# A fused attention and feed-forward layer on one core: the choice of path moved behind the fast path, and the first groups fed in another way

## The chip, the cores and the metric

The kernel runs on one core of a Trainium2 chip. A core has five engines that run side by side: TensorE (PE, matrix products), VectorE (DVE), ScalarE (ACT), GpSimd (POOL) and SyncE (SP, which only issues transfers here). The metric is the device time of one execution in microseconds. A group of transfers is issued from SP's queue or from ScalarE's queue, and an engine waits for another, or for a transfer, on a semaphore.

## The reference

The input x has shape (2, 256, 128, 128): batch, time, frequency, channels. Three residual steps follow each other, each behind a layer norm over the channels:

```
xt = _ln(x, ln_t_w, ln_t_b).transpose(0, 2, 1, 3)
x = x + _mha(xt, t_wi, t_bi, t_wo, t_bo, H_T, cm).transpose(0, 2, 1, 3)   # causal, over the 256 times
xf = _ln(x, ln_f_w, ln_f_b)
x = x + _mha(xf, f_wi, f_bi, f_wo, f_bo, H_F, bm)                         # band of 16, over the 128 frequencies
xn = _ln(x, ln_n_w, ln_n_b)
h = jax.nn.gelu(xn @ w1.T + b1, approximate=False)
x = x + (h @ w2.T + b2)
```

`_mha` is attention with four heads of 32 channels: queries, keys and values from one product with wi, scores divided by the root of 32, a mask, a softmax, the product with the values, and the product with wo. Everything is in float32. The inner width of the last step is 512.

## The kernel before

**Two paths.** A softmax is usually computed with the row's maximum subtracted. The kernel has a `shifted_path` that does so, and a `bounded_path` that leaves it out. The second is right where the weights bound the scores. The function `fold` folds the layer norm's weights into wi (`wf`), folds the biases (`bq`), and computes from these weights six sums (`tests`). They are compared with limits, and the outcome is one integer, `flag` (line 415 loads it into a register of every engine). A branch on it chooses the path (line 1263). In the runs shown the bounded path is taken.

**Groups.** The bounded path works on 128x512 tiles, called groups here: four rows of 128 tokens each. There are 128 groups of attention over time (class `OverTime`, called g0, g1 and so on below), then, in turns of eight, groups of attention over frequency (`OverBands`) and of the feed-forward step (`FeedForward`). A group goes through these methods:

- `load`: four transfers of 32 partitions each bring four groups' tokens at once (a quad).
- `statistics`: VectorE forms mean and variance (tiles `stats`, `mv`). `root_by_scalar`: ScalarE forms the inverse root as a logarithm and an exponential (`lnv`, `root`). `refine`: three small VectorE steps make it exact (`vy`, `rstd`).
- `normalize`: four VectorE instructions write the normalized tokens `xh`. `turn`: VectorE transposes blocks of 32x32 into `z`, and four transfers write z to DRAM (`turned`). `fetch`: one transfer reads it back with channels on the partitions (`xnT`). So a group is transposed by VectorE and two trips through DRAM.
- `queries_keys`, `take_query`, `take_key`: TensorE multiplies xnT with `wf`, ScalarE copies the results out as `qT` and `kT`. `values`, `take_values` give `v`.
- Scores, exponentials (`p`, by ScalarE), masks and sums (POOL), `weigh` (TensorE: sums of weights `rp` and outputs `op`), `invert`, `divide` (`oT`), `output` and `finish`.

**Order.** `run` (line 1109) writes the whole order out by hand. In one pass n of its loop it emits the steps of several groups: the scores of g(n), the queries of g(n+2), the fetch for g(n+3), the normalizing of g(n+4), the statistics of g(n+5), the roots of g(n+5). Passes below zero fill the pipeline. Instructions emitted through the wrapper `InOrder` keep this order on their engine, and an engine takes its list strictly from the front. TensorE's results go to eight banks of PSUM. The time groups use a fixed rotation of banks, the others take the next one in a ring (`turn_of_bank`).

**Start.** `load_constants` issues, on SP's queue, the small columns and rows and then the first quad (`x0`, four transfers of 256 KB), and on ScalarE's queue the weights. Then comes `fold`, then the branch. Inside the bounded path, in pass n = -4, `fold_rest` computes what is left of the folding (`wn`, `orow`, `b1`, `w1f`), and `warm` sends eight products of 128x384 that nobody reads through TensorE. All instructions that go through `InOrder` carry one line of the program in the profile (924 before), so groups of instructions are told apart by their tiles.

Of the kernel before, what the change touches and what calls it, by code (L numbers as in the profile page):

```python
# [28 lines left out]
RUN = 32  # L29
SAFE = 30.0  # L30
# [11 lines left out]
def load_constants(ctx, tc, x, t_wiT, t_woT, f_wiT, f_woT, w1T, w2T, cols, rows):  # L42
# [5 lines left out]
    k.const = const  # L48
    k.cols = const.tile([P, 16], F32, name="cols_sb")
    nc.sync.dma_start(k.cols, cols)  # L50
    k.rows = const.tile([P, 3, C], F32, name="rows_sb")
    for i in range(3):
        nc.sync.dma_start(k.rows[:, i, :], rows[i : i + 1, :].partition_broadcast(P).squeeze(1))


    k.x0 = const.tile([P, NT, NT, C], F32, name="x0")
    for i in range(NT):
        f = i // (T // P) * NT
        nc.sync.dma_start(k.x0[rows_of(i)], BoundedPath.of_times(x[0], i, slice(f, f + NT)))

    def weight(src, n, name):
        t = const.tile([P, n], F32, name=name)
        nc.scalar.dma_start(t, src)
        return t

    k.wiT = (weight(t_wiT, 3 * C, "t_wiT_sb"), weight(f_wiT, 3 * C, "f_wiT_sb"))
    k.woT = (weight(t_woT, C, "t_woT_sb"), weight(f_woT, C, "f_woT_sb"))
    k.w1T = weight(w1T, k.NI * P, "w1T_sb")
    k.w2T = const.tile([P, k.NI, C], F32, name="w2T_sb")
    nc.scalar.dma_start(k.w2T, w2T.rearrange("(j p) c -> p j c", p=P))  # L70
# [273 lines left out]
def fold(tc, k):  # L344

    nc = tc.nc
    const = k.const
    C = P  # L350
    scale = 1.0 / math.sqrt(D)
    tensor, vector, scalar = InOrder(tc, nc.tensor), InOrder(tc, nc.vector), InOrder(tc, nc.scalar)

    def col(i):
        return k.cols[:, i : i + 1]

    k.ones = const.tile([P, P], F32, name="ones")
    nc.vector.memset(k.ones, 1.0)
    k.wf, k.bq = [], []
    tests = const.tile([P, 6], F32, name="tests")  # L360
    with tc.tile_pool(name="foldp", bufs=2) as fp, tc.tile_pool(name="foldps", bufs=1, space=PSUM) as pp:
        scalar.preload_act_table_set(EXP_SET)

        bp = pp.tile([P, 2], F32, name="bp")
        for a in range(2):
            tensor.matmul(bp[:, a : a + 1], k.wiT[a][:, 0:C], col(5 * a + 1), start=True, stop=True)
        for a in range(2):
            c0 = 5 * a
            wf = const.tile([P, 3 * C], F32, name=f"wf{a}")
            vector.tensor_scalar(wf[:, 0:C], k.wiT[a][:, 0:C], col(c0), scale, ALU.mult, ALU.mult)  # L370
            vector.tensor_scalar(wf[:, C : 3 * C], k.wiT[a][:, C : 3 * C], col(c0), None, ALU.mult)
            bq = const.tile([P, 1], F32, name=f"bq{a}")
            vector.tensor_scalar(bq, bp[:, a : a + 1], col(c0 + 2), scale, ALU.add, ALU.mult)
            k.wf.append(wf)
            k.bq.append(bq)
        brs = []
        for a in range(2):
            brp = pp.tile([1, P], F32, name=f"brp{a}")
            tensor.matmul(brp, k.bq[a], k.ident, start=True, stop=True)
            br = fp.tile([1, P], F32, name="br")  # L380
            scalar.copy(br, brp)
            brs.append(br)

        for a in range(2):
            wf, wo = k.wf[a], k.woT[a]
            br = brs[a]
            gk = pp.tile([P, P], F32, name="gk", tag=f"gk{a}")
            tensor.matmul(gk, wf[:, C : 2 * C], wf[:, C : 2 * C], start=True, stop=True)
            gq = pp.tile([P, P], F32, name="gq", tag=f"gq{a}")
            tensor.matmul(gq, wf[:, 0:C], wf[:, 0:C], start=True, stop=False)  # L390
            tensor.matmul(gq, br, br, start=False, stop=True)
            gs = fp.tile([P, P], F32, name="gs")
            scalar.copy(gs, gk)
            vector.tensor_tensor(gs, gq, gs, ALU.mult)
            for h in range(H):
                r = rows_of(h)
                vector.tensor_reduce(tests[r, 3 * a : 3 * a + 1], gs[r, r], AX.X, ALU.add)
            for j, w in ((1, wf[:, 2 * C : 3 * C]), (2, wo)):
                sq = fp.tile([P, P], F32, name="sq")
                scalar.activation(sq, w, AF.Square, accum_out=tests[:, 3 * a + j : 3 * a + j + 1])  # L400
        tp = pp.tile([P, 6], F32, name="tp")
        tensor.matmul(tp, k.ones, tests, start=True, stop=True)
        ok = fp.tile([P, 6], F32, name="ok")
        for a in range(2):
            vector.tensor_scalar(
                ok[:, 3 * a : 3 * a + 1], tp[:, 3 * a : 3 * a + 1], SAFE * SAFE / (C * (C + 1)), None, ALU.is_le
            )
            vector.tensor_scalar(
                ok[:, 3 * a + 1 : 3 * a + 3], tp[:, 3 * a + 1 : 3 * a + 3], LARGE, None, ALU.is_le
            )  # L410
        allok = fp.tile([P, 1], F32, name="allok")
        vector.tensor_reduce(allok, ok, AX.X, ALU.min)
        flag = const.tile([P, 1], I32, name="flag")
        vector.tensor_copy(flag, allok)
    return nc.values_load(flag[0:1, 0:1], min_val=0, max_val=1)


# [10 lines left out]
class Group:  # L428
# [91 lines left out]
    def fetch(self):  # L520
        path = self.path
        self.xnT = path.work.tile([P, NT * P], F32, name="xnT")
        path.sync.dma_start(self.xnT, self.turned.rearrange("c a i x -> (c a) (i x)"))

# [404 lines left out]
class BoundedPath:  # L929
    def __init__(self, ctx, tc, k):  # L930
# [12 lines left out]
        self.sync = InOrder(tc, tc.nc.sync)  # L943
        self.dram = ctx.enter_context(tc.tile_pool(name="turns", bufs=3, space=DRAM))
        self.zero = 0.0
        self.once = once = ctx.enter_context(tc.tile_pool(name="once", bufs=1))
        self.eps = once.tile([P, 1], F32, name="eps")
# [121 lines left out]
    def fold_rest(self):  # L1069

        k, tensor, vector, scalar = self.k, self.tensor, self.vector, self.scalar
        C = P

        def col(i):
            return k.cols[:, i : i + 1]

        k.wn, k.orow = [], []
        for a in range(2):
            c0 = 5 * a

            bp = self.bank([P, 1], "bp")
            tensor.matmul(bp, k.wiT[a][:, 2 * C : 3 * C], col(c0 + 1), start=True, stop=True)
            bv = self.small.tile([P, 1], F32, name="bv")
            scalar.activation(bv, bp, AF.Identity, bias=col(c0 + 4))
            wn = self.once.tile([P, C], F32, name=f"wn{a}")
            scalar.mul(wn, k.woT[a], -1.0)
            k.wn.append(wn)
            orow = self.once.tile([P, C], F32, name=f"orow{a}")
            scalar.activation(orow, k.ones, AF.Copy, scale=bv)
            op = self.bank([P, C], "op")  # L1090
            tensor.matmul(op, orow, k.woT[a], start=True, stop=True)
            vector.tensor_tensor(orow, op, k.rows[:, a, :], ALU.add)
            k.orow.append(orow)
        b1p = self.bank([P, k.NI], "b1p")
        for j in range(k.NI):
            tensor.matmul(b1p[:, j : j + 1], k.w1T[:, j * P : (j + 1) * P], col(11), start=True, stop=True)
        k.b1 = self.once.tile([P, k.NI], F32, name="b1")
        vector.tensor_tensor(k.b1, b1p, k.cols[:, 12 : 12 + k.NI], ALU.add)
        k.w1f = self.once.tile([P, k.NI * P], F32, name="w1f")
        scalar.activation(k.w1f, k.w1T, AF.Copy, scale=col(10))  # L1100

    def warm(self):


        for _ in range(8):
            bank = self.bank([P, 3 * P], "warm")
            self.tensor.matmul(bank, self.k.ones, self.k.wf[0], start=True, stop=True)

    def run(self, x, out):
# [24 lines left out]
        self.scalar.preload_act_table_set(EXP_SET)  # L1134
        for n in range(-12, len(groups) + 2):
# [13 lines left out]
            if old is not None or new is not None:  # L1149
                time_scores(old, new)  # L1150
                b = self.banks
                Attention.place = dict(yp=b["b0"], rp=b["b3"], op=b["a1"], qp=b["a2"], kp=b["b1"], vp0=b["b0"], vp1=b["b2"])
            else:
                Attention.place = {}
# [19 lines left out]
            do_at(n + 3, OverTime, "fetch")  # L1174
# [8 lines left out]
            do_at(n + 4, OverTime, "normalize", "turn")  # L1183
# [11 lines left out]
            if n == -4:  # L1195
                self.fold_rest()
                self.warm()
# [4 lines left out]
            if bands[2] or turn:  # L1202
                do(n - 2, "output", "finish")
            do(n - 1, "divide")
# [15 lines left out]
            if n < 0:  # L1220
                do_at(n + 5, OverTime, "root_by_scalar", "refine")
            do_at(n, OverTime, "bias")
# [81 lines left out]
```

## Time and profile before

| what | us |
| --- | --- |
| median of three runs | 2664.97 |
| lowest and highest | 2662.14, 2665.03 |
| profiled execution: its own time | 2662.95 |
| its span | 2661.2 |
| TensorE busy in the span | 2630.1 (99%) |
| VectorE, ScalarE, POOL busy | 2140.1, 1841.8, 1947.3 |
| first queries of g0 begin | 28.27 |

The profile is one execution. Times count from the start of its span. A row of the timeline gives the start, the length, the engine, the line, the operation, the tile that it writes and those that it reads, shapes and count. Square brackets give the idle time of that engine before the row, and what ended it. PEld is the loading of weights into TensorE, which overlaps the products. Matmuls are pipelined and their ends are modelled, so starts are the safer numbers. A float32 product appears as two records.

### The profile page before, as it was taken

To read this page: it belongs to the slowest core of one execution; us is meant where nothing else is said; L and a number is where in the kernel's file an instruction comes from. 1 tells how busy PE (TensorE), PEld (TensorE's weight loads), DVE (VectorE), ACT (ScalarE), POOL (GpSimd) and SP (SyncE) were. 2 spreads that over 40 slices of the span, in tenths; PEclk is the share of its full clock that TensorE was granted. 3 is DMA by queue.
4 is the path that set the end of the run, shared out by engine and by line. 5 is a ranking of instruction groups with operands and counts; after the bars stand their busy time and mean duration, and the time that the engine had idled before them with its cause. 6 is when DMAs were issued, how large, how long until landed. Compare 5 with 4: busy or idle time off the path is not lost.

```text
span 2661.2 us, 156426 instructions
## 1 busy us (share of the span) xinstructions
PE 2630.1 (99%) x68662; PEld 1930.4 (73%) x68662; DVE 2140.1 (80%) x6429; ACT 1841.8 (69%) x3562; POOL 1947.3 (73%) x2297
## 2 busy tenths in 40 slices
PE   7999999999999999999999999999999999999998
PEld 5667667666676668778777687777777877777777
DVE  6988888888888897977868779678687796886874
ACT  6898999989989874664755746647557466475573
POOL 4999999999999986756667667666676676666762
PEclk9999999999999999999999999999999999999999
DMA  6655555555556454444444444444444454544533
GB/s 147 159 155 149 152 153 153 150 151 157 149 154 153 121 129 120 124 122 126 118 118 126 122 118 126 120 125 118 123 125 119 117 129 113 133 118 121 127 95 82
DMA packets 471510, 347.08 MB, mean 130 GB/s; under 512 B 43296, under 2 KB 405152, under 8 KB 470816
## 3 DMA queue, kind: packets, MB, share of 16 engines
q1 hardware_dynamic: 469568, 335.92, 49.0%
q8 instruction: 540, 8.85, 1.5%
q10 hardware_dynamic: 1248, 1.05, 0.2%
q14 instruction: 154, 1.26, 0.2%
HBM read 169.03 MB, written 167.77 MB: 127 GB/s over the span
## 4 chain that ended last, share of the span: by engine, by line
PE 86%; DVE 10%; DMA 2%; SPq 0%; issue 0%; ACT 0%; DVEq 0%; ACTq 0%
PE bank L924 86%; DVE xh L924 2%; DVE bank L924 2%; DVE z L924 1%; DVE u L924 1%; DVE oT L924 1%; DVE stats L924 1%; DVE x L924 1%; DMA xnT<-turned 1%; DMA turned<-z 1%; SPq L924 0%; DVE mv L924 0%; DMA x<-in_x 0%; DMA rows_sb<-in_rows 0%; ACT p L924 0%
## 5 line engine op out<-in xcount | busy, mean ns | idle before, releaser
L924 ACT ACTIVATE hT<-bank,b 128x512 f32<-128x512 f32 x512 | 346.9, 688 | 527.0 <-PE bank L924 496.3
L924 POOL TENSOR_SCALAR_AFFINE_SELECT pf<-pf 128x512 f32<-128x512 f32 x768 | 476.8, 635 | 178.5 <-ACT pf L924 152.2
L924 PEld LDWEIGHTS bank<-w2T_sb,hT 128*32 128x32 f32 x16384 | 498.2, 110 | 22.9 <-issue 16.7
L924 PE MATMUL bank<-xnT,w1f 128*32 128x512 f32 x4096 | 510.0, 592 | 0.0
L924 PE MATMUL bank<-w2T_sb,hT 128*32 128x128 f32 x16384 | 504.0, 273 | 0.2 <-ACT hT L924 0.2
L924 PE MATMUL bank<-xnT,wf 128*32 128x512 f32 x4096 | 492.5, 592 | 3.5 <-ACT p L924 3.0
L924 ACT ACTIVATE p<-bank 128x512 f32<-128x512 f32 (+1 forms) x1024 | 430.4, 495 | 65.0 <-PE bank L924 64.6
L924 POOL TENSOR_SCALAR_AFFINE_SELECT p<-p 128x1024 f32<-128x1024 f32 (+2 forms) x384 | 363.6, 947 | 81.2 <-ACT p L924 72.9
L924 DVE TENSOR_SCALAR xh<-x,mv,rstd 128x160 f32<-128x160 f32 x1040 | 404.4, 431 | 9.7
L924 PEld LDWEIGHTS bank<-wf,xnT 128*32 128x32 f32 x8192 | 243.6, 110 | 144.0 <-issue 103.2
L924 DVE TENSOR_TENSOR res<-bank,res 128x512 f32<-128x512 f32 x256 | 170.5, 666 | 218.8 <-PE bank L924 192.0
L924 PEld LDWEIGHTS bank<-xnT,w1f 128*32 128x32 f32 x4096 | 247.2, 110 | 128.2 <-issue 114.9
L924 POOL TENSOR_TENSOR p<-p,p 128x512 f32<-128x512 f32 x256 | 323.9, 1287 | 10.7
L924 DVE BATCH_NORM_STATS2 stats<-x 128x6 f32<-128x128 f32 x1536 | 329.5, 277 | 0.2 <-DMA x<-in_x 0.2
L924 POOL TENSOR_SCALAR rstd<-mv 128x4 f32<-128x4 f32 x248 | 56.3, 227 | 369.1 <-DVE mv L924 368.3
L924 PE MATMUL bank<-qT,kT 32*64 32x80 f32 (+4 forms) x16384 | 314.3, 273 | 2.4 <-ACT p L924 1.0
L924 PEld LDWEIGHTS bank<-qT,kT 32*64 32x64 f32 x16384 | 271.3, 131 | 54.5 <-ACT kT L924 50.3
L924 ACT ACTIVATE pf<-bank 128x512 f32<-128x512 f32 x512 | 266.7, 602 | 46.7 <-PE bank L924 44.1
L924 PE MATMUL bank<-wn,oT 128*32 128x128 f32 x8192 | 283.4, 274 | 0.7 <-DVE oT L924 0.7
L924 DVE STREAM_TRANSPOSE z<-xh 128x512 f32<-128x512 f32 x384 | 273.3, 712 | 13.2
L924 PE MATMUL bank<-wf,xnT 128*32 128x128 f32 x8192 | 276.7, 273 | 0.0
L924 POOL TENSOR_TENSOR rstd<-rstd,mhalf 128x4 f32<-128x4 f32 x248 | 256.6, 1035 | 20.7
(102 smaller groups left out, 3806.0 us busy)
## 6 DMA issues: line engine op xcount, KB each, us to landing
turned<-z SPq DMA_DIRECT2D x1536, 64.0 KB, 2.7
xnT<-turned SPq DMA_DIRECT2D x384, 256.0 KB, 3.1
x<-in_x SPq DMA_DIRECT2D x128, 256.0 KB, 4.4
x<-res SPq DMA_DIRECT2D x256, 128.0 KB, 2.6
x<-x SPq DMA_DIRECT2D x128, 256.0 KB, 4.2
out<-res SPq DMA_DIRECT2D x256, 128.0 KB, 2.5
w1T_sb<-in_w1T ACTq DMA_DIRECT2D x1, 256.0 KB, 5.7
w2T_sb<-in_w2T ACTq DMA_DIRECT2D x1, 256.0 KB, 7.0
```

The costliest lines, as they stand in the source:

```text
L924: return self.tc.keep_in_program_order(emit(*args, **kwargs))
```

## The change

The branch is moved to the end. The bounded path always runs. The shifted path follows only where the flag is zero, and writes the output again. The six sums and the flag are computed during the feed-forward stage.

Four other things change with it:

- The first quad is loaded group by group: g0's tokens first, then g1's, then g2's and g3's together. `cols` moves to ScalarE's queue, where the load of the activation tables stands behind the first weight.
- The first four groups (`TURNED`) are not transposed through DRAM. `normalize_flat` writes xh densely, `turn_by_tensor` multiplies it with the identity on TensorE, and ScalarE copies the result from PSUM into `xnT`.
- The folding is spread over VectorE, POOL and ScalarE and over several passes of the loop (`fold`, `fold_products`, `fold_biases`, `squares`, `fold_outputs`, `fold_rows`, `fold_hidden`). The second `wf`, `wn` and `w1f` are now made by POOL.
- The eight warm products use the identity and ones instead of a folded weight, and run at the very start: three, then the two small products of `fold_products`, then five.

```diff
+TURNED = 4
 def load_constants(...):
-    nc.sync.dma_start(k.cols, cols)
+    scalar.dma_start(k.cols, cols)
+    k.x0 = const.tile([P, NT, NT, C], F32, name="x0")
+    def tokens(g, n):
+        for i in range(NT):
+            f = i // (T // P) * NT + g
+            sync.dma_start(k.x0[rows_of(i), :, g : g + n], BoundedPath.of_times(x[0], i, slice(f, f + n)))
...
+    tokens(0, 1)
+    t_wi = weight(t_wiT, 3 * C, "t_wiT_sb")
+    scalar.preload_act_table_set(EXP_SET)
+    tokens(1, 1)
+    k.wiT = (t_wi, weight(f_wiT, 3 * C, "f_wiT_sb"))
+    k.woT = (weight(t_woT, C, "t_woT_sb"), weight(f_woT, C, "f_woT_sb"))
     k.rows = const.tile([P, 3, C], F32, name="rows_sb")
...
+    tokens(2, 2)
     k.w1T = weight(w1T, k.NI * P, "w1T_sb")
...
+    def normalize_flat(self):
+        path = self.path
+        self.xh = path.work.tile([P, NT, P], F32, name="xh", bufs=2)
+        for i in range(NT):
+            path.vector.tensor_scalar(
+                self.xh[:, i], self.src()[:, i], self.mv[:, i, 0:1], self.rstd[:, i : i + 1], ALU.subtract, ALU.mult
+            )
+
+    def turn_by_tensor(self, bank):
+        path = self.path
+        self.turned = path.bank([P, NT, NT, D], "turn", bank)
+        for i in range(NT):
+            path.tensor.matmul(
+                self.turned[:, i].rearrange("p i q -> p (i q)"), self.xh[:, i], path.k.ident, start=True, stop=True
+            )
+        self.xnT = path.work.tile([P, NT * P], F32, name="xnT")
+        path.scalar.copy(self.xnT.rearrange("p (i t q) -> p t i q", i=NT, q=D), self.turned)
...
+    def fold(self, a, engine):
+        engine.tensor_scalar(wf[:, 0:C], k.wiT[a][:, 0:C], col, 1.0 / math.sqrt(D), ALU.mult, ALU.mult)
+        engine.tensor_scalar(wf[:, C : 3 * C], k.wiT[a][:, C : 3 * C], col, None, ALU.mult)
...
+    def squares(self):
+        for a in range(2):
+            tensor.matmul(brp[0:1, a], k.bq[a], k.ident, start=True, stop=True)
+        scalar.copy(br, brp[0:1])
+        for a in range(2):
+            tensor.matmul(gk[:, a], wf[:, C : 2 * C], wf[:, C : 2 * C], start=True, stop=True)
+        scalar.copy(self.gs[:, 0], gk)
+        for a in range(2):
+            tensor.matmul(gq[a], wf[:, 0:C], wf[:, 0:C], start=True, stop=False)
+            tensor.matmul(gq[a], br[:, a], br[:, a], start=False, stop=True)
+            scalar.copy(self.gs[:, 1, a], gq[a])
...
+    def fold_outputs(self):
+        for a in range(2):
+            tensor.matmul(bp[:, a : a + 1], k.wiT[a][:, 2 * C :], k.cols[:, c0 + 1 : c0 + 2], start=True, stop=True)
+        for a in range(2):
+            scalar.activation(bv[:, a : a + 1], bp[:, a : a + 1], AF.Identity, bias=k.cols[:, c0 + 4 : c0 + 5])
+            scalar.activation(k.orow[a], k.ones, AF.Copy, scale=bv[:, a : a + 1])
+            tensor.matmul(self.orowp[:, a], k.orow[a], k.woT[a], start=True, stop=True)
+            self.gpsimd.tensor_scalar(k.wn[a], k.woT[a], -1.0, None, ALU.mult)
...
     def run(self, x, out):
+        self.warm(range(3))
+        self.fold(0, self.vector)
+        self.fold(1, self.gpsimd)
+        self.fold_products()
+        self.warm(range(3, 8))
         for n in range(-12, len(groups) + 2):
...
-            do_at(n + 3, OverTime, "fetch")
+            if n + 3 >= TURNED:
+                do_at(n + 3, OverTime, "fetch")
...
-            do_at(n + 4, OverTime, "normalize", "turn")
+            if n + 4 < TURNED:
+                do(n + 4, "normalize_flat")
+            else:
+                do_at(n + 4, OverTime, "normalize", "turn")
+            if n == -4:
+                groups[0].turn_by_tensor(4)
...
-            if n == -4:
-                self.fold_rest()
-                self.warm()
+            if n == -5:
+                self.fold_biases()
...
+            if n == len(groups):
+                self.bounded = self.nc.values_load(self.flag[0:1, 0:1], min_val=0, max_val=1)
             do(n - 1, "divide")
...
+            if n == -5:
+                self.squares()
+                self.fold_outputs()
+            if n == -4:
+                self.fold_rows()
+            for i in range(2):
+                if n == ff[i]:
+                    self.test(i)
+            if n == ff[2]:
+                self.verdict()
...
             do_at(n + 2, OverTime, "values", "take_values")
+            if 0 < n + 3 < TURNED:
+                groups[n + 3].turn_by_tensor(2 if n == -2 else self.banks["a1"])
+            if n == -2:
+                self.fold_hidden()
...
-    bounded = fold(tc, k)
-    with tc.If(bounded > 0) as cmp:
-        bounded_path(tc, k, x, out)
-    with cmp.Else():
+    bounded = bounded_path(tc, k, x, out)
+    with tc.If(bounded < 1):
         shifted_path(tc, k, x, out)
```

`test` and `verdict` hold the sums and comparisons that stood in `fold`. The third and fourth feed-forward groups run `test` (one product, four sums and two squares each), and the fifth runs `verdict`, whose one matmul is called `tp`.

## The prediction

> **What bounds the kernel now.** The page comes first: the busy line, then the chain that ended last.
>
> ```profile
> PE 2630.1 (99%) x68662; PEld 1930.4 (73%) x68662; DVE 2140.1 (80%) x6429; ACT 1841.8 (69%) x3562; POOL 1947.3 (73%) x2297
> ...
> PE 86%; DVE 10%; DMA 2%; SPq 0%; issue 0%; ACT 0%; DVEq 0%; ACTq 0%
> ```
>
> TensorE is the bound nearly everywhere, and the change leaves the order of its work untouched after the fourth group (the two kernels' lists of TensorE instructions agree there but for one matmul). So only the start can move. The timeline of the start, by engine (start, length, engine, instruction, wait before it):
>
> ```profile
> 13.09 0.15 DVE L924 CAST flag<-allok 128x1 int32<-128x1 f32 x1
> ...
> 14.33 0.87 DVE L924 BATCH_NORM_STATS2 stats<-x 128x6 f32<-128x128 f32 x4 [0.25 <-DMA x<-in_x]
> ...
> 23.51 0.34 PEld L924 LDWEIGHTS bank<-wf,ones 128*128 128x128 f32 x1 [0.30 <-issue]
> ...
> 24.15 0.34 PEld L924 LDWEIGHTS bank<-wf,ones 128*128 128x128 f32 x1 [0.30 <-issue]
> ...
> 24.79 2.94 PEld L924 LDWEIGHTS bank<-wf,ones 128*128 128x128 f32 x9 [0.30 <-issue]
> ```
>
> Nothing of the tokens is touched before the flag of 13.09 is read. The eight warm matmuls from 20.80 run 0.64 us per half (23.51 to 24.15), then 0.33 (2.94 over 9): the clock doubles near 25, 4.3 us after they began, although the clock shown by stretches is 1.00. Then TensorE alone:
>
> ```profile
> 20.80 7.53 PE L924 MATMUL bank<-wf,ones 128*128 128x384 f32 x16
> 28.27 1.93 PE L924 MATMUL bank<-xnT,wf 128*32 128x512 f32 x16
> ...
> 34.14 1.92 PE L924 MATMUL bank<-xnT,wf 128*32 128x512 f32 x16 [1.15 <-ACT p L924]
> ...
> 40.22 1.92 PE L924 MATMUL bank<-xnT,wf 128*32 128x512 f32 x16 [1.83 <-ACT p L924]
> ...
> 47.01 1.93 PE L924 MATMUL bank<-xnT,wf 128*32 128x512 f32 x16
> ...
> 54.95 2.23 PE L924 MATMUL bank<-xnT,wf 128*32 128x512 f32 x16 [0.56 <-DMA xnT<-turned]
> ```
>
> Each xnT,wf row opens a group's queries and keys: g0 at 28.27, then 5.87, 6.08, 6.79, 7.94 later. From g4 on nothing differs between the builds, so the question is when g4 starts, now 54.95. Finally ScalarE's rows of the first groups:
>
> ```profile
> 25.51 0.30 ACT L924 ACTIVATE lnv<-mv,eps 128x4 f32<-128x4 f32 x1 [4.82 <-DVE mv L924]
> 25.84 0.20 ACT L924 ACTIVATE root<-lnv 128x4 f32<-128x4 f32 x1
> 29.40 0.69 ACT L924 ACTIVATE qT<-bank,bq 128x512 f32<-128x512 f32 x1 [3.36 <-PE bank L924]
> ```
>
> The roots of g1 and g2 were done before g0's queries existed: the turn through DRAM left VectorE free to run ahead. That is what the change disturbs.
>
> **What the Trainium skill says.** "TensorE: Matmul & The Clock Gate", What's actually happening: the clock runs at half until a busy window of 3413 ns has passed, windows being free-running; the 4.3 us above agree. Same page, Architectural detail: ScalarE and VectorE are strict FIFO. The trace agrees: qT above stands behind both roots. "ScalarE: Activation LUTs", What ACT_TABLE_LOAD costs: an ACTIVATE without pointer operand takes 186 ns + 0.833 N, 0.61 for N = 512; kT's copy took 0.58.
>
> **The change, step by step** (times from the span's start; X is the moment g0's xnT is ready).
>
> *To the end of the warm matmuls.* Gone from the front: the squares' tests, the flag, the branch (13.09 to 13.9). Tokens of g0 come first; four 64 KB issues of 0.44 (turned<-z, 1.77 for 4) and 2.7 to land give about 5. TensorE needs only ident: 1.6. Three warm matmuls at 1.28 end at 5.5; bp needs f_wi, which landed 3.5 after its issue; it is now behind t_wi and a table load of 1.28, so issued 1.7 to 3.0, landing 5.2 to 6.5. Five more warm matmuls cost 3.2 fast, 6.4 slow: end 9.5 to 12.5. I take 10.0, the clock having risen around 7.
>
> *To X.* TensorE's queue now holds brp, gk, gq, the outputs' fold, and only then g0's turn. ScalarE in order: br 0.25, gs of 256 0.31, two gs 0.27, bv 0.24, orow 0.39, bv, orow, with a handover of about 0.1 to 0.2 each: 3.9 after the block. Two products at 0.3 (0.59 cold, 6.75 to 7.34, halved), one of them hidden; four turning products 1.2 (the trace has no such turn; 0.9 if weight loads hide, 2.4 cold); the copy of xnT 0.61 to 0.69. X = 10.0 + 6.1 = 16.1, against 28.27: 12.2 earlier. Group 0's own normalizing (tokens 5, stats 0.87 + 0.36, root, xh: about 9.5) is hidden under it.
>
> *g0 to g1: here most of it goes back.* In ScalarE's list the roots of g1 and g2 now stand behind g0's xnT and before g0's qT, and VectorE's list has xh of g1 before the stats of g2. So, after X: root g1 0.54 (15.57 to 16.11); rstd 0.60; two orow adds 0.4; xh g1 4 x 0.35 = 1.4 + 0.1 (unshown shape: 0.40 apiece at 160, about 0.2 in wf, so 0.8 to 1.6); stats g2 0.75 + 0.36; lnv, root 0.62: root g2 at X + 4.8. Only then qT to X + 5.5, kT X + 6.0. The next root (g3) waits likewise: rstd g2 0.6, xh 1.5, stats 1.1, root 0.6: X + 8.6; behind it v to X + 9.3, xnT of g1 X + 9.9, two p of 0.48: X + 10.9 frees the bank for g1's queries. Interval 10.8 instead of 5.87. TensorE's turn of g1 (1.2) and b1p (0.9) lie inside these waits.
>
> *g1 to g2*: turn 1.2 ahead of the scores, which start at 3.9 instead of 2.7; the p after them keep 3.3: 7.2 instead of 6.08. *g2 to g3*: turn g3, less 0.5 of TensorE's wait for p (44.85): 7.6 instead of 6.79. *g3 to g4*: the 0.56 for xnT goes (z of g4 is ready near X + 17.6, DRAM turn and fetch 4.3 + 4.9 by the slowest here, X + 27, needed at X + 33), ScalarE's backlog costs about 0.2: 7.6 instead of 7.94. Together 33.2: g4 at 49.3, 5.65 earlier.
>
> *Costs elsewhere.* Tests in the feed-forward stage: four squares on ScalarE, two products and eight reduces on VectorE, hidden under TensorE (hT rows idle 527 us in all); tp on TensorE itself costs 0.3. Without that cover about 3 in all. POOL's wf1, wn, w1f replace ScalarE and VectorE work, POOL being idle there until 35; uncovered, w1f would cost its 0.71. SP's and the other engines' flag load waits for a flag long set; VectorE's stands in its last idle (4.88). The jump over the unused path exists now too. Loads: ten quads now issue back to back ahead of g4's turn, 2.5 MB at the 205 GB/s of the first 14 us, 12 us, done near 25, before that turn. Bank numbers differ by one in the first band groups: within 1 either way, taken as 0.
>
> Sum: -5.65 + 0.3 = -5.35 from the profiled execution, 2662.95 us (span 2661.2): 2657.6. That execution was 2.0 under the median, 2664.97, and its clock rose early in its possible 3.4 us; I add 0.4: 2658.0.
>
> **Rivals.** *Nearly all of it stays* (2653.6): if the roots do not hold back qT, because xh is short and VectorE keeps ahead, intervals grow only by the turns: 26.1 + 3 x 0.9 = 28.8, g4 at 44.9. For it: ScalarE has slack. Against: FIFO and the two orders.
>
> *The clock spoils it* (2659 to 2664): bp's one-column products break the dense window, so the block ends at 12.5 (2.5 later), or the idle gaps of X + 2.8 to 5.6 and 8.7 to 10.9 bring half clock back for one group (3 to 4). For it: from 5.7 to 10.5 now TensorE is busy and still slow. Against: neither gap holds a whole window.
>
> *Slower*: one mechanism, the half clock lasting from the start through g1. Price: block and products to X 4.8; TensorE's work from X to g2, 11.3, doubles, 5 of it in waits: 6.3. Together 11.1: g4 at 60.4, 2669; it passes +0.2% (2670.3) once g2 runs slow too (another 3): 2672. The block of eight warm matmuls speaks against it.
>
> *The fold still gates the start*: excluded, the flag's load stands behind the last product in TensorE's list.
>
> **How the numbers follow.** Likeliest 0.53 (own range 2655 to 2660); nearly all 0.17; clock 0.25; slower mechanism 0.05. A measurement here tells 0.2%, 5.3 us, from no change: faster means under 2659.6. Faster: 0.17 + 0.47 + 0.04 = 0.68; same 0.27; slower 0.05. Range 2651.5 to 2664.5, leaving out the low end of the second and the worst of the last two.
>
> **What would show it.** Right: first xnT,wf row near 16; ScalarE's second lnv before qT waiting about 3.5 for VectorE's mv; second xnT,wf about 11 after the first, g4 near 49, then the old 7.08 rhythm. Wrong: qT right behind the first queries (rival one); matmuls of the first groups at twice their old spacing (clock); a wait on x or xnT by DMA before g8, which would put the loads in the way.

## The result and the profile after

The median of 12 runs is 2658.91 us (2652.79 to 2662.68), against 2665.65 for the kernel before in the same session. The ratio is 0.9976, 95% interval 0.9968 to 0.9983. A second session gave 2655.24 against 2663.36, ratio 0.9971 (0.9959 to 0.9982). The prediction was 2658.0. The total came out; two of its parts did not. A start that won less than predicted, and a gain in a place that the prediction called unchanged, made up the difference.

The page's busy line and the chain that ended last, after:

```profile
PE 2629.9 (99%) x68694; PEld 1924.4 (72%) x68694; DVE 2135.9 (80%) x6423; ACT 1843.1 (69%) x3562; POOL 1951.8 (73%) x2302
...
PE 86%; DVE 12%; issue 0%; DMA 0%; ACT 0%; POOL 0%; SPq 0%; ACTq 0%; DVEq 0%
```

TensorE is still the bound. The timeline of the start after, TensorE's warm products and the first touch of the tokens (start, length, engine, instruction, wait before it):

```profile
5.59 0.38 PE L877 MATMUL bank<-cols_sb,f_wiT_sb 128*128 128x1 f32 x2 [0.23 <-DMA f_wiT_sb<-in_f_wiT]
5.84 3.47 PE L877 MATMUL bank<-ident,ones 128*128 128x384 f32 x10
...
5.98 0.87 DVE L877 BATCH_NORM_STATS2 stats<-x 128x6 f32<-128x128 f32 x4 [0.57 <-DMA f_woT_sb<-in_f_woT]
```

Statistics begin at 5.98, not 14.33. The last ten warm records take 3.47, where the first six took 3.73: the clock had risen in between. Then the first queries and keys of g0 to g4, on TensorE, after:

```profile
16.12 2.97 PE L877 MATMUL bank<-xnT,wf 128*32 128x512 f32 x16 [0.68 <-ACT xnT L877]
...
25.65 3.32 PE L877 MATMUL bank<-xnT,wf 128*32 128x512 f32 x16 [1.88 <-ACT p L877]
...
34.70 3.06 PE L877 MATMUL bank<-xnT,wf 128*32 128x512 f32 x16 [2.02 <-ACT p L877]
...
44.76 1.93 PE L877 MATMUL bank<-xnT,wf 128*32 128x512 f32 x16
...
51.96 1.90 PE L877 MATMUL bank<-xnT,wf 128*32 128x512 f32 x16
```

g0 starts 12.15 earlier than before. g4 starts only 2.99 earlier. The intervals are 9.53, 9.05, 10.06 and 7.20 (before: 5.87, 6.08, 6.79, 7.94). And the first three rows take about 3 us, where the same sixteen products took 1.92 before. ScalarE's rows of that time, after:

```profile
15.48 0.58 ACT L877 COPY xnT<-bank 128x512 f32<-128x512 f32 x1 [1.69 <-PE bank L877]
...
16.30 0.20 ACT L877 ACTIVATE root<-lnv 128x4 f32<-128x4 f32 x1
19.61 0.30 ACT L877 ACTIVATE lnv<-mv,eps 128x4 f32<-128x4 f32 x1 [3.11 <-DVE mv L877]
...
20.05 0.67 ACT L877 ACTIVATE qT<-bank,bq 128x512 f32<-128x512 f32 x1
...
23.06 0.30 ACT L877 ACTIVATE lnv<-mv,eps 128x4 f32<-128x4 f32 x1 [1.86 <-DVE mv L877]
```

The root of g2 holds up qT of g0 for 3.11, as the prediction said, and the root of g3 then holds up v and the next xnT for 1.86. The slow rows have another cause. A table by stretches of the kernel after: length, busy time of PE, PEld, DVE, ACT and POOL with counts, then TensorE's granted clock (1.00 is full, 0.50 half), DMA share, GB/s:

```profile
11.46:14.87 3.41, 2.53 (x18) 2.13 (x18) 0.00 (x0) 1.48 (x5) 0.00 (x0) 1.00 1.05 236
14.87:18.28 3.41, 2.73 (x16) 0.87 (x18) 1.68 (x9) 0.99 (x3) 0.00 (x0) 0.50 1.07 223
21.69:25.11 3.42, 2.08 (x43) 1.61 (x41) 2.75 (x18) 2.02 (x7) 0.00 (x0) 1.00 0.55 115
25.11:28.52 3.41, 2.87 (x16) 0.79 (x20) 1.28 (x9) 2.15 (x4) 1.10 (x1) 0.50 0.00 0
31.93:35.34 3.41, 1.39 (x44) 0.82 (x32) 2.20 (x7) 2.59 (x9) 1.09 (x1) 1.00 0.11 21
35.34:38.76 3.42, 3.42 (x36) 1.68 (x32) 3.31 (x15) 2.06 (x5) 3.30 (x4) 0.50 0.43 66
933.05:936.46 3.41, 1.70 (x64) 1.13 (x60) 2.60 (x7) 2.60 (x7) 3.26 (x5) 1.00 0.37 75
936.46:939.88 3.42, 3.42 (x52) 2.53 (x44) 3.35 (x13) 1.14 (x4) 3.35 (x4) 0.50 0.24 81
```

The rows come in pairs: a window of 3.41 in which TensorE was idle for 0.9 to 2.0, and the next one at half clock. The queries of g0 and g1 fall into a slow one, those of g2 (from 34.70) for the most part. The fourth pair lies at the change from time groups to band groups.

For g0 the slow row costs nothing, because the interval hangs on the roots. The kernel after was profiled a second time (called e10_after_again below). There g0's products ran at full clock, and g1 still came 9.53 later:

```profile
16.17 1.92 PE L877 MATMUL bank<-xnT,wf 128*32 128x512 f32 x16 [0.68 <-ACT xnT L877]
...
25.70 3.64 PE L877 MATMUL bank<-xnT,wf 128*32 128x512 f32 x16 [1.22 <-ACT p L877]
```

So where did the time go? The table splits the span at the first queries of attention groups, in us. Counting attention groups only, g128 is the first band group and g255 the last. The recorded expectations call g255's start that of the last feed-forward group. The feed-forward groups between the band groups lie in the fourth column.

| | to g4 | g4 to g127 | g127 to g128 | g128 to g255 | rest | span |
| --- | --- | --- | --- | --- | --- | --- |
| before | 54.95 | 872.91 | 12.72 | 1645.13 | 75.49 | 2661.2 |
| after | 51.96 | 874.44 | 14.40 | 1642.25 | 75.05 | 2658.1 |
| after, second session | 52.58 | 872.22 | 12.72 | 1639.94 | 74.65 | 2652.1 |

The first column is 2.4 to 3.0 less. The fourth is 2.9 to 5.2 less, and nothing there was meant to change. Single late waits of 0.2 to 0.8, at other groups in each trace, scatter the second and fourth columns by a microsecond or two.

### The profile page after: what moved, and what is told of

It is laid out like the page before. It is cut to its first block, busy times and chain, and to the rows that moved or that the text cites. A ratio compares the mean times of both kernels' runs of the same rounds, so it can differ in the third digit from the quotient of the medians.

```text
span 2658.1 us, 156476 instructions
## 1 busy us (share of the span) xinstructions
PE 2629.9 (99%) x68694; PEld 1924.4 (72%) x68694; DVE 2135.9 (80%) x6423; ACT 1843.1 (69%) x3562; POOL 1951.8 (73%) x2302
## 4 chain that ended last, share of the span: by engine, by line
PE 86%; DVE 12%; issue 0%; DMA 0%; ACT 0%; POOL 0%; SPq 0%; ACTq 0%; DVEq 0%
PE bank L877 86%; DVE xh L877 3%; DVE bank L877 2%; DVE u L877 1%; DVE oT L877 1%; DVE z L877 1%; DVE stats L877 1%; DVE x L877 1%; DVE mv L877 0%; DMA xnT<-turned 0%; ACT p L877 0%; DMA f_wiT_sb<-in_f_wiT 0%; DMA turned<-z 0%; POOL rstd L877 0%; POOL pf L877 0%
## 5 line engine op out<-in xcount | busy, mean ns | idle before, releaser
L877 PE MATMUL bank<-xnT,wf 128*32 128x512 f32 x4096 | 498.0, 596 | 4.6 <-ACT p L877 3.9
L877 DVE TENSOR_SCALAR xh<-x,mv,rstd 128x160 f32<-128x160 f32 (+1 forms) x1040 | 403.1, 430 | 9.6
L877 PEld LDWEIGHTS bank<-xnT,w1f 128*32 128x32 f32 x4096 | 239.7, 110 | 132.5 <-issue 116.7
L877 PE MATMUL bank<-qT,kT 32*64 32x80 f32 (+4 forms) x16384 | 304.4, 271 | 1.6 <-ACT p L877 1.1
L877 PEld LDWEIGHTS bank<-qT,kT 32*64 32x64 f32 x16384 | 261.1, 131 | 53.4 <-ACT kT L877 50.0
L877 ACT ACTIVATE pf<-bank 128x512 f32<-128x512 f32 x512 | 267.7, 602 | 42.5 <-PE bank L877 33.2
```

The costliest lines, as they stand in the source:

```text
L877: return self.tc.keep_in_program_order(emit(*args, **kwargs))
```

## The experiments

Theory 1: the roots in ScalarE's list make g0 to g1 long. Theory 2: idle gaps bring the half clock back and make the next two intervals long. Theory 3, formed after the first four runs, is on the fourth column. All times are medians; each session had its own runs of the kernel before (2663.36 to 2664.02).

| kernel | us | ratio to before (95%) | g0 | g4 | g128 to g255 |
| --- | --- | --- | --- | --- | --- |
| e1_branch_only | 2661.39 | 0.9992 (0.9983 to 1.0) | 30.35 | 56.29 | 1639.76 |
| e2_dram_turn | 2656.59 | 0.9970 (0.9959 to 0.9981) | 21.78 | 51.52 | 1640.57 |
| e3_roots_first | 2651.84 | 0.9956 (0.9942 to 0.9969) | 16.61 | 49.27 | 1640.01 |
| e4_fill | 2653.52 | 0.9964 (0.9950 to 0.9978) | 16.52 | 50.11 | 1640.14 |
| e5_roots_fill | 2653.70 | 0.9961 (0.9948 to 0.9975) | 15.57 | 45.73 | 1641.45 |
| e6_guarded | 2660.00 | 0.9986 (0.9980 to 0.9993) | 16.34 | 52.71 | 1643.65 |
| e7_turn_two | 2653.75 | 0.9959 (0.9946 to 0.9973) | 16.17 | 47.31 | 1642.42 |
| e8_fill_switch | 2650.88 | 0.9949 (0.9935 to 0.9963) | 16.43 | 46.57 | 1642.28 |
| e9_two_arms | 2660.80 | 0.9989 (0.9982 to 0.9996) | 16.60 | 52.43 | 1646.19 |
| e11_guarded_again | 2659.72 | 0.9986 (0.9979 to 0.9992) | 17.92 | 50.90 | 1642.60 |
| e12_two_arms_again | 2660.78 | 0.9989 (0.9983 to 0.9996) | 16.75 | 51.62 | 1647.29 |

e10_after_again is the second session of the tables above. The medians of e3, e4, e5 and e7 cannot be told apart, and the intervals of all four overlap that of the second session of the kernel after. What is said of them below rests on the traces, one for each kernel. The code cuts are shortened.

**e1_branch_only.** The kernel before with the branch behind:

```diff
-    bounded = fold(tc, k)
-    with tc.If(bounded > 0) as cmp:
-        bounded_path(tc, k, x, out)
-    with cmp.Else():
+    fold(tc, k)
+    bounded = bounded_path(tc, k, x, out)   # loads the flag in its last pass
+    with tc.If(bounded < 1):
```

> The kernel before with one edit: the branch is moved to the end, the sums and the flag stay at the front. Theory (the tokens, not the flag, gate the start once the branch is gone): in the kernel before, the first statistics start at 14.33, right after the tokens land, and ScalarE's fold work stands behind the first root. So the first queries stay at 27.9 to 28.3 and the time is the same as before, within 0.5 us. Rival (the flag gates the start): the 0.8 us between flag (13.09) and first work (13.9) and the second table load go, the first queries begin near 26.5 and the time is 1.5 to 2 us less, half of the whole gain.

Both missed. The first queries came 2.1 later than before, at 30.35, and still the time fell by 2.3, with an interval that touches no change. The timeline of this kernel shows the delay, on VectorE and TensorE:

```profile
14.52 0.29 DVE L923 BATCH_NORM_STATS2 stats<-x 128x6 f32<-128x128 f32 x1 [4.28 <-DMA x<-in_x]
...
15.58 0.72 DVE L923 TENSOR_REDUCE tests<-gs 32x1 f32<-32x32 f32 x4
...
16.44 0.56 PE L923 MATMUL tp<-tests,ones 128*128 128x6 f32 x2 [5.52 <-DVE tests L923]
```

Without the branch between them, the statistics moved ahead of the sums in VectorE's list. The sums wait behind the tokens (4.28), and TensorE's whole fold waits for the sums (5.52). So the branch alone buys nothing at the start: the sums have to leave the front too, and the tokens have to come first. What it bought lies between g128 and g255, 1639.76 against 1645.13. e2, e3 and e4 came to the same 1640, which speaks against chance; this was the first hint at theory 3.

**e2_dram_turn.** The kernel after with `TURNED = 0`.

> The kernel after with one edit: no group is turned by TensorE, all go through DRAM as before; tokens first, spread folding and the late branch stay. Theory (what made the first intervals long is the turn by TensorE with the orders that come with it): the first queries begin near 18.2 (z done 10.7, four transfers to 12.5 and landed near 15.5, fetched near 18.2), 2.1 later than in the kernel after, but the intervals go back to about 5.9, 6.1, 6.8, 7.9 and g4 starts at 45 to 47 instead of 51.96, the time is 2652 to 2655, 4 to 7 us under the kernel after. TensorE idles from 14.3 to 18.2, so g0 may run at half clock, 1.5 us, which is in that range. Rival (the long intervals belong to TensorE's half clock, and the turn has nothing to do with it): intervals of 8 to 10 again, g4 near 52 to 54, time 2659 to 2661.

g0 came at 21.78, not 18.2, and the time of 2656.59 missed the 2652 to 2655. The intervals were 8.16, 7.59, 6.80 and 7.19, the first two in part under half clock, and g4 stood at 51.52, hardly better than with the turns. The timeline of this kernel, VectorE:

```profile
9.93 1.13 DVE L877 TENSOR_SCALAR xh<-x,mv,rstd 128x160 f32<-128x160 f32 x3 [0.91 <-DMA rows_sb<-in_rows]
14.09 0.44 DVE L877 TENSOR_SCALAR xh<-x,mv,rstd 128x160 f32<-128x160 f32 x1 [3.02 <-DMA x<-in_x]
```

`normalize` for the DRAM way reads 160 columns of tokens per row, 32 more than the group's own. The fourth row reaches into g3's tokens, which landed last. So "tokens group by group" and "turn by TensorE" need each other: only the dense `normalize_flat` can use g0's tokens alone. The theory's intervals were right in direction; its gain was eaten by this wait and the half clock that TensorE's 6.74 us of idling brought.

**e3_roots_first.** The kernel after, reordered:

```diff
...
             if n == -5:
+                do(0, "normalize_flat")
+                do(1, "statistics")
                 self.squares()
+                do(1, "root_by_scalar")
                 self.fold_outputs()
+                do(1, "refine", "normalize_flat")
+                do(2, "statistics"); do(3, "statistics")
             if n == -4:
                 self.fold_rows()
+                do(2, "root_by_scalar", "refine", "normalize_flat")
+                do(3, "root_by_scalar", "refine")
```

> The kernel after with the order changed: statistics of g1, g2 and g3 stand ahead of the normalizing of g2 on VectorE, and the roots of g1 (before the outputs' fold), g2 and g3 (right behind g0's xnT) on ScalarE. Theory 1 (roots hold back g0's qT, the prediction's step): no wait of 3.1 and 1.9 for mv in ScalarE's list after g0's xnT, qT comes right behind the first queries near 18, and the interval from g0 to g1 falls from 9.53 to 6.5 to 7.5. Theory 2 (half clock makes the next two intervals long): those stay at 8 to 10 wherever the clock falls, at 7 to 7.6 where it does not. With both, g4 starts near 48 to 49, 3 us earlier, time about 2656. Rival (the turns' own work on TensorE and ScalarE, 1.2 and 0.6 a group, makes all three long): g0 to g1 stays above 9.

Theory 1 holds. ScalarE's rows of this kernel:

```profile
17.21 0.20 ACT L877 ACTIVATE root<-lnv 128x4 f32<-128x4 f32 x1
18.61 0.69 ACT L877 ACTIVATE qT<-bank,bq 128x512 f32<-128x512 f32 x1 [1.20 <-PE bank L877]
```

qT now waits for its own product. g0 to g1 fell from 9.53 to 7.74; 6.5 to 7.5 was expected, and g0's queries ran at half clock. The next two intervals were 7.66, at full clock throughout, and 10.07, with g2's queries at half clock (3.62 for the sixteen). g4 came at 49.27. That fits theory 2, and other traces settle it without any change of order. e11_guarded_again and e12_two_arms_again (below) have the order of the kernel after. In e11 both intervals ran at full clock and took 7.65 and 8.38. In e12 the first of them fell under half clock and took 9.78; the second, at full clock, took 8.38:

```profile
36.05 1.92 PE L877 MATMUL bank<-xnT,wf 128*32 128x512 f32 x16 [2.02 <-ACT p L877]
...
44.43 1.93 PE L877 MATMUL bank<-xnT,wf 128*32 128x512 f32 x16
```

So the half clock costs 1.4 to 2.1 in g1 to g2 and 1.6 to 1.7 in g2 to g3. At full clock 1.6 remains over the old 6.08 and 6.79 in each; the turn's products are 1.16 of it.

**e4_fill.** The kernel after with nine products that nobody reads, for example:

```diff
+            if n == -1:
+                self.warm([3] * 3)
+            if n == 0:
+                self.warm([self.banks["b0"]] * 3)
             do_at(n + 2, OverTime, "queries_keys", "take_query", "take_key")
```

> The kernel after with nine more products of ones and identity, 128x384, that nobody reads, in TensorE's idle times: one before the outputs' fold and one after g0's turn, one before g1's turn, three before g1's queries, three before g2's queries (0.64 each at full clock); the small products b1p write other columns of the same bank. Theory 2 (idle times bring the half clock back): no half clock after 8, the queries and keys of g0, g1 and g2 take 1.9 instead of 3.0, 3.3 and 3.1, intervals about 8.5, 7.8, 8.6 instead of 9.53, 9.05 and 10.06, g4 near 48.5 to 49.5, time about 3 us under the kernel after. Rival (ScalarE's list sets the pace, TensorE waits for p anyway): full clock, and the same intervals within 0.5; time as the kernel after or 1 us more.

The first queries of g0, g1, g2 and g3 in this kernel:

```profile
16.52 1.92 PE L877 MATMUL bank<-xnT,wf 128*32 128x512 f32 x16
...
26.84 1.92 PE L877 MATMUL bank<-xnT,wf 128*32 128x512 f32 x16
...
34.54 1.92 PE L877 MATMUL bank<-xnT,wf 128*32 128x512 f32 x16
...
42.91 1.93 PE L877 MATMUL bank<-xnT,wf 128*32 128x512 f32 x16
```

The half clock is gone: 1.92 in every row, and the intervals 9.05 and 10.06 became 7.70 and 8.37. That agrees with theory 2. The first interval grew to 10.32, which was missed: the three products before g1's queries waited 0.54 for VectorE to read their bank and ended late. g4 at 50.11.

**e5_roots_fill.** e3 and e4 together, with one product instead of three before g1's queries and none before g1's turn.

> Both cures at once: the order of e3_roots_first, and six products that nobody reads in TensorE's idle times (one before the outputs' fold, one after g0's turn, one before g1's queries, three before g2's queries). Theory (root order and half clock are two separate losses that add): no half clock in the first 50 us, intervals of 6.9, 7.7, 8.4 and 7.2, g4 at 46.5 to 47 against 49.27 with the order alone and 50.11 with the fill alone; time 2649. Rival (one loss only, the fill hides what the order cures): g4 at 49 again, time 2652.

The trace is as expected: intervals of 6.88, 7.70, 8.38 and 7.20, full clock, g4 at 45.73, span 2647.9. The two losses add: from g0 to g4 the kernel after takes 35.84, e3 3.2 less, e4 2.3 less, e5 5.7 less. The median of five runs, 2653.7, does not show the further gain over e3; its profiled run was its fastest.

**e7_turn_two.** e5 with `TURNED = 2`.

> As e5_roots_fill, but only g0 and g1 are turned by TensorE, g2 and g3 go through DRAM. Theory (each turn by TensorE that is not needed costs its 1.2 on TensorE and its 0.6 on ScalarE in the interval it stands in): z of g2 ready near 20, fetched and landed near 28, before its queries near 30; intervals 6.9, 6.5, 7.2, 7.2, g4 at 44 to 45, time 2647. Rival (the transfers are late behind the loads of the next tokens, as with no turn at all, where g0's tokens of the last row landed at 14.1 and g0's queries waited 6.7): a wait of 2 or more for xnT by DMA before the queries of g2 or g3, g4 at 47 or later.

Worse in the trace (g4 at 47.31), level in the median, and by another wait than either side named. g1 to g2 took 10.27. The timeline of this kernel, VectorE, then ScalarE:

```profile
26.66 0.88 DVE L877 BATCH_NORM_STATS2 stats<-x 128x6 f32<-128x128 f32 x4 [3.29 <-DMA x<-in_x]
...
27.84 0.30 ACT L877 ACTIVATE lnv<-mv,eps 128x4 f32<-128x4 f32 x1 [2.22 <-DVE mv L877]
```

The transfers of z, issued at 20.05, stood ahead of the loads of g4's tokens in SP's queue. The tokens came late, g4's root with them, and v of g1 stands behind that root. The same pattern as in theory 1, now fed by a transfer. The wait also brought the half clock, from 29.17 to 32.59: the six records of the filling products before g2's queries took 3.55, where e4's took 2.20.

**e8_fill_switch.** e5 with two more such products where TensorE waits at the change to band groups.

> As e5_roots_fill, with two more such products at the change from time groups to band groups, one before the last group's scores and one before the outputs behind them, where TensorE waits 1.05 and 0.66. Theory (whether this gap costs the clock depends on how a window of 3.41 us falls over it: it did in two of six traces, for 1.7): the last time interval is 12.7 to 12.9 in every run, the time 0 to 1 us under e5_roots_fill. Rival: the added products delay the last scores, the interval is 13.3 or more, time 0.6 us over e5_roots_fill.

The interval was 12.86, full clock. Of 14 traces in this study, three lost the clock in this place (14.40 instead of 12.72), this kernel's did not; most of the others did not either, so one trace shows no gain. Its median, 2650.88, is the lowest of all kernels. Its interval, 0.9935 to 0.9963, lies under that of the kernel after in the first session (0.9968 to 0.9983) and touches that of the second.

**e6_guarded and e11_guarded_again.** Theory 3 concerns the semaphore updates: signals with which a finished instruction tells other engines so. In the trace, TensorE's matmuls between 1000 and 2580 us carry 5702 of them before and 1716 after.

```diff
+    with tc.If(go > 0):            # go: a constant one, loaded at the start
+        flag = bounded_path(tc, k, x, out)
+    bounded = values_load(flag)
     with tc.If(bounded < 1):
```

> The kernel after with one edit: the bounded path stands again inside a branch, whose condition is a constant one written at the start, and the flag is read behind it. Theory (3): in the traces of the kernel before, TensorE's matmuls between 1000 and 2580 us carry 5702 semaphore updates, in all kernels with the late branch 1716, and the stretch from the first band group to the last feed-forward group took 1645.1 before and 1639.8 to 1642.3 after; the branch around the path makes these updates, each costs up to 25 ns where short score products follow each other. Then this kernel has about 5700 again, the stretch takes 1644 to 1646, and the time is 4 to 6 us over the kernel after, about 2663 to 2665, equal to the kernel before. Rival (the difference in this stretch is chance of late transfers): about 1700 updates or, with 5700, a stretch of 1640 to 1642, and a time of 2659 to 2660.

> e6_guarded a second time, now on one chip with e9_two_arms. In its first trace the stretch from the first band group to the last feed-forward group took 1643.65, 3.7 over that of e10_after_again, in scattered single waits of TensorE that the profile puts down to issue (3.3 us in 8 places, 0.2 in e10_after_again, 1.9 in the first trace of the kernel after). Theory (such waits fall by chance, the guard costs only its flag load at the start, under 1 us): issue waits under 2 us in this trace, the stretch 1640 to 1642, the time 2655 to 2658. Rival (the guard makes them): 3 us of issue waits again, 1643 to 1645, time 2660.

The updates did not return (1719 and 1721), so theory 3 fell in that form. The time was 2660.0 and 2659.7, against 2658.91 and 2655.24 for the kernel after in its two sessions; the intervals overlap. In the traces, TensorE's waits by what ended them between 945 and 2590 us had 3.3 and 1.5 us put down to issue (the engine waited for nothing that the profile shows). The line of e6:

```profile
PE bank L877 <- issue: 3.3, 8, 0.8
```

The kernel after had 1.9 and 0.2 in its two traces, and e8, without a guard, 3.6. So the waits are not tied to the guard by these runs. Neither expectation of e11 fits whole: its trace was short of the rival's numbers, its median was the rival's. What a guard of one arm costs over the kernel after (1 to 5 us by these medians), and why, stays open.

**e9_two_arms and e12_two_arms_again.** e6 with the shifted path in a second arm, as in the kernel before:

```diff
-    with tc.If(go > 0):
-        flag = bounded_path(tc, k, x, out)
-    bounded = values_load(flag)
-    with tc.If(bounded < 1):
+    with tc.If(go > 0) as cmp:
+        bounded_path(tc, k, x, out)
+    with cmp.Else():
         shifted_path(tc, k, x, out)
```

This kernel leaves out the use of the flag: the bounded path is always taken.

> As e6_guarded, but the branch on the constant one has two arms, as in the kernel before: the bounded path in one, the shifted path in the other, and no second branch behind. In e6_guarded TensorE's matmuls carried 1719 updates between 1000 and 2580 us, as in the kernel after, so a branch around the path does not make them. In the compiled program of this kernel 13,629 matmuls carry an update, 13,592 in the kernel before, some 8,040 in the kernel after and in e6_guarded. Theory (3b): the two arms make the updates and the updates make the stretch longer. Then about 5700 updates in that time, the stretch from the first band group to the last feed-forward group takes 1644.5 to 1646 with score products 25 ns apart more often, and the time is 2663 to 2665, 4 over e6_guarded (2660.0). Rival (updates are free, the stretch differs by chance of late transfers): 5700 updates, a stretch of 1640 to 1643, time 2660.

> The kernel after itself, on the same chip as e9_two_arms, for a direct comparison. Theory 3b: 3 to 5 us under e9_two_arms, about 2659. Rival: within 1 us of it. The clock rises again at another place of its 3.41 us windows, so which of the first groups loses it differs from the first trace, but one to three of the first five windows after 11 us are at half.

> e9_two_arms a second time, on the same chip as e11_guarded_again; the two differ by the second arm and with it by the updates on TensorE's matmuls (5699 against 1719 between 1000 and 2580 us). Theory 3b (updates cost 25 ns apiece where short score products follow each other, 0.3 us a block of eight band groups, 5 us in all): the same pattern of 0.05 to 0.15 more in every band group, the time 3 to 5 us over e11_guarded_again. Rival (updates are hidden, or the one-armed guard costs as much): within 1 us of e11_guarded_again.

The updates returned (5699 and 5694), and with them the long stretch, 1646.19 and 1647.29. The three traces with two arms have 1645.1 to 1647.3 there, the eleven others 1639.8 to 1643.7. e10, the kernel after once more, took 2655.24, 5.6 under e9 on the same chip, a little more than expected; two of its first five windows after 11 us ran at half clock, as expected. Group for group e9 exceeds e10 by 0.03 to 0.15 in most band groups and falls short by about 0.25 over each feed-forward run, 0.3 net for a block of eight, sixteen times. By the same pattern the kernel before exceeds e1, and e12 exceeds e11. The place is the short score products of the band groups. Groups of instructions by shape, 1000 to 2580 us: busy time, mean ns, idle time before. The kernel before:

```profile
L924 PE MATMUL bank<-pf,ones 128*32 128x512 f32 x936 | 128.4, 603 | 3.5 <-DVE oT L924 3.3
L924 PE MATMUL bank<-qT,kT 32*64 32x80 f32 x7552 | 124.1, 244 | 0.0
```

The kernel after, first session:

```profile
L877 PE MATMUL bank<-qT,kT 32*64 32x80 f32 x7592 | 115.2, 240 | 0.5 <-issue 0.5
```

e9_two_arms:

```profile
L877 PE MATMUL bank<-qT,kT 32*64 32x80 f32 x7552 | 123.9, 244 | 0.0
```

e10_after_again:

```profile
L877 PE MATMUL bank<-pf,ones 128*32 128x512 f32 x944 | 131.2, 603 | 6.8 <-DVE oT L877 6.8
L877 PE MATMUL bank<-qT,kT 32*64 32x80 f32 x7616 | 115.0, 240 | 0.0
```

The same products in e11_guarded_again, then in e12_two_arms_again, which differ by the second arm alone:

```profile
L877 PE MATMUL bank<-qT,kT 32*64 32x80 f32 x7616 | 115.2, 240 | 0.1
...
L877 PE MATMUL bank<-qT,kT 32*64 32x80 f32 x7552 | 124.0, 244 | 0.0
```

These products take 9.1 us more with two arms (124.1 before against 115.0 in e10). Of that about 3.3 seems to be covered, because TensorE otherwise waits that much longer for oT (6.8 against 3.5). What is left is 5.8, and the table says 5.2 for before against e10. From a group's first score product to the product behind its scores, the median is 0.994 to 0.995 in the three traces with two arms and 0.896 to 0.897 in all others, the guard of one arm included. So the second arm makes the scores slower.

That the updates are the means is likely, not shown by an experiment of its own. For it: in e9 six band groups, the second to the seventh, carry no more updates on their scores than in e10, and they are level with it. The 41 with three to five more are 0.047 behind (median), the 81 with six or more 0.099. But the delays do not come right behind the products that carry an update, so how an update would delay them is open.

In the total the clean comparison is weak. Against the guard of one arm the medians of the two-armed kernels are higher by only 0.8 and 1.1, where 3 to 5 was expected, and the intervals overlap. e11's profiled run was 2.4 under its own median, so its trace may not hold all of the guard's cost.

## Why the prediction was right, and where it was wrong

**To X: right, with some luck.** X was 16.1, and g0's queries began at 16.12. The warm products ended at 9.3 instead of 10.0, and the part behind them took 6.8 instead of 6.1: ScalarE's list needed 4.5 after the block, not 3.9.

**g0 to g1: right in mechanism, 1.3 too long in size.** The wait for mv was 3.11, about 3.5 predicted. The dense xh took 1.11 for four, not 1.5, and it stands twice in the chain. The half clock of g0's queries has no part in the 9.53, for e10 has the same interval at full clock.

**g1 to g2 and g2 to g3: wrong.** The prediction has 7.2 and 7.6; measured 9.05 and 10.06. At full clock they take 7.65 and 8.38 (e11), so the turns' steps were short by 0.45 and 0.8, and the clock added 1.4 and 1.7. The failing sentence is "neither gap holds a whole window". None has to. The Trainium skill, "TensorE: Matmul & The Clock Gate", HAM oscillation — how this bites in real kernels, gives "no PE-idle gaps >~3.4µs" as the abstract rule. In the table by stretches above, windows whose longest gap was 0.8 to 2.0, and in which TensorE was busy for 1.39 to 2.53 of 3.41, were followed by a slow one: the measurement decides. The same page, What's actually happening, says that the windows are free-running; the traces agree: every half-clock stretch before the last few us of a kernel begins and ends on a grid of 3.41, whose phase differs from run to run. The rival "the clock spoils it" had the mechanism and the price, 3 to 4; the clock cost 3.1 in the first trace and 3.6 in the second, spread over two intervals instead of one group.

**g3 to g4: about right**, 7.20 against 7.6. Together the lead at g4 was 2.4 to 3.0 instead of 5.65. At full clock the four intervals add up to 32.8, against 33.2 predicted, because their errors cancel. What was missing at g4, 2.7 in the first trace, is the clock.

**"From g4 on nothing differs between the builds": wrong.** The order of the instructions is the same; their semaphore updates are not. This is the step that failed in the other direction. The late branch has one arm and the two-armed one is gone. With it some 4000 updates left TensorE's matmuls between 1000 and 2580 us, and the stretch of the band groups became 2.9 to 5.2 shorter. e1 shows it with the branch alone, e9 and e12 by putting the two arms back.

**Costs elsewhere.** `tp` and the sums: 0.3 predicted. The feed-forward stretch that holds them took 62.99 and 62.87 in the kernel after, 62.31 in e1: 0.6 to 0.7. The bank numbers by one: taken as nothing, and e1 with the old numbers agrees with e10 within 0.2. The work moved to POOL was done by 9.7 and held nothing up in these timelines. The loads were done by 25, as predicted, but the rate was loosely named: the first 14 us before moved 164 GB/s on average, and 205 to 243 only from 2 to 12 us. The "ten quads" are ten transfers of 256 KB. Not foreseen: the slow window at the change to band groups, 1.7 in the first trace, nil in the second.

So 2658.0 was met by luck: about 3 us too much at the start and 2.9 to 5.2 us that no step had forecast in the band groups cancelled.

## What to carry to other kernels

Compare not only the order of two builds but also what each instruction signals: here a second arm around a long body cost 0.1 us in each group of 64 short products. A prologue that wins time can lose it again to the clock, so count idle times well under the clock's window too, and take several traces, for the phase of the windows differs. And when a step is moved ahead on an engine with a strict order, list what then stands behind it: here the roots of later groups held up g0's own steps (9.53 with them, 6.88 without them at full clock).

## What was not expected of the hardware

- The clock fell to half after windows of 3.41 us in which TensorE was busy for 41% to 92% of the time (the 92% at 10.25 to 13.66 in e11), and it stayed there for one window, two (23.02 to 29.84 in e10) or three (13.66 to 23.90 in e11). Other windows with as little as 41% kept full clock (34.03 to 37.45 in e12, with a gap of 2.02 as in the kernel after). So no share of busy time divides them in these traces, and what does is not settled.
- In the kernel before, the clock reads 1.00 in stretches before 25 us although products ran at half speed: the first change of clock on record there is at 25.11, and nothing earlier is shown.
- A DMA issued from ScalarE's queue behind the load of its activation tables was not held up by it: f_wi was issued at 1.75, while the table load ran from 1.72 to 3.00.
